# Three of the seven block products of q and k split a second time, in a two-layer graph network on one core

## The chip, the core and the metric

The kernel runs on one core of a Trainium2 chip. The metric is device time in microseconds (us). The kernel before takes 2371.41 us, the median of three runs (2370.97 to 2373.28). TensorE (PE) does matrix products into PSUM, VectorE (DVE) and ScalarE (ACT) work on SBUF and PSUM, GpSimd (POOL) on SBUF, and SyncE (SP) issues nearly all DMAs. Each engine works through its own queue in order.

## What is computed

128 graphs of 128 nodes with 512 features, in float32. Cut to what matters:

```python
# layer 0: attention over 8 heads of 64 features, masked by adj
q, k, v = x @ Wq + bq, x @ Wk + bk, x @ Wv + bv
scores = einsum('bqhd,bkhd->bhqk', q, k) / sqrt(64) + (1 - adj) * -1e9
out = einsum('bhqk,bkhd->bqhd', softmax(scores), v)
x = layernorm(x + out @ Wo + bo)
# layer 1: additive attention
h = x @ W;  s1, s2 = h @ a[:512], h @ a[512:]
e = leaky_relu(s1[:, :, None] + s2[:, None, :]) * adj
x = layernorm(x + elu(softmax(e) @ h + beta * h))
```

## The kernel before

**Tiling.** A batch is one graph; two batches are a group g (64 groups, b0 and b1), two groups a step of four batches. The five products with a 512x512 weight are done by groups in halves: weight and x are cut into 2x2 blocks, and seven block products with sums of blocks on both sides take the place of eight (Strassen's scheme in Winograd's form). The weights' sums are made once (`weight_sum`, L220), those of x, of the attention's output and of layer 1's aggregate by GpSimd (`block_sum`, L260; tiles tx, tw, th). `product` (L300) does one of the seven. For q and k it covers two groups at once: four matmuls of 256 columns (L325). For v, w (the output product with Wo) and h (with W) it is two matmuls for one group (L318).

**Adding up.** Products 1, 6, 5, 3 accumulate in one PSUM tile (`main`), 7 and 4 in another (`side`), and 2 stands alone for q and k. Between them the running sum is read out: `take_part` (L364) copies it to SBUF on ScalarE (on VectorE for w, with the residual added), `add_block` (L380) adds a later part on VectorE. A product that accumulates further waits until the running sum has been read out.

**Attention.** `scores` (L388) makes q k^T, `mask` (L402) scales and masks it on VectorE into tile s, `row_max` (L411), `exps` (L415) and `row_inv` (L424) prepare the softmax, `normalise` (L428) writes it on ScalarE into a second tile sb, laid out in 32-column pieces. It is transposed by a write to DRAM (`attn_write`), a read back in blocks (`attn_read`, tile ab) and a 32x32 block transpose on VectorE (`turn_attn`, L458). `attend` (L467) multiplies by v (PSUM tile po), `attend_evict` (L479) brings it to SBUF (oT).

**Layer 1.** Statistics of the first norm (`bn_stats`, `bn_aggr`, `inv_std` with a power on GpSimd), `row_product` (L518, two per batch, for s1 and s2), `norm_c` (L536, VectorE, into tile x1), the edge weights (`edge`, `leaky`, `edge_exp`, `weights`), `aggregate` (L655, PSUM tile pz, four matmuls of 128 columns), the h products, and ELU: `elu_exp` (ScalarE), `elu_max` and `elu_sum` (VectorE, into tile u), the last norm `norm_f` and `store`.

**x and the weights.** `load_blocks` (L78) fetches x in 32-row pieces, `turn_x` (L246) transposes it by 32x32 blocks on VectorE. It reads every fourth feature (a stride of four elements), so that wq, wk and wv can be loaded with four whole rows per partition (`load_turned`, L103, one DMA each).

**What sets the order.** No scheduler: `rows` (L765), `last_rows` (L908) and the lists in `other` (L1043) give every piece of every group a place, `lay` (L1235) shifts it by STEP for each pair of groups, and the pieces are issued sorted by place (L1284). The order on each engine is thus written out by hand; waits come from the tiles' uses.

Of the kernel before, what the change touches and what calls it, by code (L numbers as in the profile page):

```python
# [13 lines left out]
P = 128  # L14
Q = 32
# [3 lines left out]
STEP = 72.624  # L19
# [3 lines left out]
def gnn_two_layers(  # L23
# [70 lines left out]
    def load_x(b):  # L94
        t = wk2.tile([P, D], F32, tag="x", name=f"x_{b}", bufs=4)
        nc.sync.dma_start(out=t, in_=x[b])
        return t
# [5 lines left out]
    def load_turned(t, src):  # L103
        nc.sync.dma_start(out=t, in_=src.rearrange("(p m) f -> p m f", m=NC))
# [15 lines left out]
    load_turned(wq_sb, wq)  # L120
# [28 lines left out]
    nc.gpsimd.memset(mhalf, -0.5)  # L149
    bq_c, bk_c, bv_c = (bias_c[:, i * NC : (i + 1) * NC] for i in range(3))  # L150
# [7 lines left out]
    def load_later():  # L158
        nc.gpsimd.dma_start(out=adj_sb, in_=adj)
        later["beta"] = broadcast(cpool, beta, 1, "beta_b")  # L160
        later["bo"] = broadcast(cpool, bo, D, "bo_b")
        for j in range(2):
            a_j = a1[j * D : (j + 1) * D].rearrange("f o -> (f o)")
            later["a", j] = broadcast(wk2, a_j, D, "uf")
# [18 lines left out]
    def wa_column(j, c):  # L183
        t = wk2.tile([P, D], F32, tag="u", name=f"wa_t_{j}_{c}", bufs=1)
# [35 lines left out]
    def weight_sum(name, n, eng):  # L220
# [5 lines left out]
        s2, s3, s4 = (sums[name][:, i] for i in range(3))  # L226
        if n == 3:
# [7 lines left out]
        left[name] = {1: a11, 2: a12, 3: s4, 4: a22, 5: a21, 6: s2, 7: s3}  # L235


    right, tx, qT, kT, vb, y, hp, main, side, oT, zT, xr = ({} for _ in range(12))
# [7 lines left out]

    def turn_x(g, t):
        nc.vector.transpose(  # L248
            xT_all[:, :, t, g % 2, :].rearrange("p m (b r) -> p b m r", r=Q),
            xblk[g][:, t].rearrange("p b (c m) -> p b m c", c=Q),  # L250
        )
# [7 lines left out]

    def block_sum(name, g, n):  # L260

        if name == "x":
            b11, b12, b21, b22, (t1, t2, t3, t4) = x_blocks(g % 2)
        else:
            src = oT if name == "w" else zT
            b11, b12 = src[g * G][:, :2], src[g * G + 1][:, :2]
            b21, b22 = src[g * G][:, 2:], src[g * G + 1][:, 2:]
            if (name, g) not in tx:
                tx[name, g] = grp.tile(
                    [P, 4, 2, N], F32, tag=f"t{name}", name=f"t{name}_{g}", bufs=1  # L270
                )
            t1, t2, t3, t4 = (tx[name, g][:, i] for i in range(4))
        to, a, b = {1: (t1, b12, b11), 2: (t2, b22, t1), 3: (t3, b22, b12), 4: (t4, b21, t2)}[n]
        nc.gpsimd.tensor_tensor(to, a, b, ALU.subtract)  # L274
        if name != "x":
            right[name, g] = {1: b11, 2: b21, 3: b22, 4: t4, 5: t1, 6: t2, 7: t3}

    def factor(name, g, n):

        if name in "qkv":  # L280
            b11, b12, b21, b22, (t1, t2, t3, t4) = x_blocks(g % 2 if name == "v" else None)
            return {1: b11, 2: b21, 3: b22, 4: t4, 5: t1, 6: t2, 7: t3}[n]
        if (name, g) in right:
            return right[name, g][n]

        src = oT if name == "w" else zT
        return {1: src[g * G][:, :2], 2: src[g * G][:, 2:]}[n]
# [52 lines left out]
    def whole(name, b):  # L340
        out = OUT[name]
        if b not in out:
# [18 lines left out]
    def plain_take(b):  # L361
        nc.vector.tensor_tensor(whole("w", b), pl["w", b], xr[b], ALU.add)

    def take_part(name, g, n, i, j):  # L364
# [5 lines left out]
        elif name == "w":  # L370
            res = xr[g * G + j][:, i * HF : (i + 1) * HF]
            nc.vector.tensor_tensor(dst, src, res, ALU.add)  # L372
        else:
            for m in range(2):
                nc.scalar.activation(  # L375
                    dst[:, m, :], src[:, m, :], AF.Identity,
                    bias=BIAS[name][:, 2 * i + m : 2 * i + m + 1],
                )

    def add_block(name, g, n, i, j):  # L380

        src, dst = region(name, g, n), block(name, g, i, j)
        nc.vector.tensor_tensor(dst, src, dst, ALU.add)


    psc, s_t, nmax, rsum, rinv, sb, scr_t, ab = ({} for _ in range(8))
# [15 lines left out]
    def mask(b, j):  # L402
        if j == 0:
            s_t[b] = wk2.tile([P, H, N], F32, tag="s", name=f"s_{b}")
        nc.vector.scalar_tensor_tensor(  # L405
            s_t[b][:, j * HP : (j + 1) * HP, :], psc[b][j], SCALE,
            amask.rearrange("p (o n) -> p o n", o=1).broadcast_to([P, HP, N]),
            ALU.mult, ALU.add,
        )

    def row_max(b):  # L411
        nmax[b] = st.tile([P, H], F32, tag="nmax", name=f"nmax_{b}")
        nc.vector.tensor_reduce(nmax[b], s_t[b], AX.X, ALU.max, negate=True)  # L413

    def exps(b, k):  # L415
        if k == 0:
            rsum[b] = st.tile([P, H], F32, tag="rsum", name=f"rsum_{b}")
        for h in range(2 * k, 2 * k + 2):
            nc.scalar.activation(  # L419
                s_t[b][:, h, :], s_t[b][:, h, :], AF.Exp, bias=nmax[b][:, h : h + 1],  # L420
# [7 lines left out]
    def normalise(b, k):  # L428

        if k == 0:  # L430
            sb[b] = wk2.tile([P, 4, H, Q], F32, tag="sb", name=f"sb_{b}", bufs=1)
        for h in range(2 * k, 2 * k + 2):
            nc.scalar.mul(  # L433
                sb[b][:, :, h, :], s_t[b][:, h, :].rearrange("p (b c) -> p b c", c=Q),
                rinv[b][:, h : h + 1],
            )

    def attn_write(b):
        scr_t[b] = scr.tile([P, 4, H * Q], F32, tag="scr", name=f"scr_{b}")
        nc.sync.dma_start(out=scr_t[b], in_=sb.pop(b).rearrange("p b h c -> p b (h c)"))  # L440
# [15 lines left out]
    attnT, po, x1, stats, mv, ve, rstd, s12, s12n = ({} for _ in range(9))  # L456

    def turn_attn(b, half):  # L458
        if half == 0:
# [54 lines left out]
    def inv_std(g, name, i=None):  # L514
        t, r = pair(rstd, (name, g), f"rstd{name}"), part_of(i)
        nc.gpsimd.tensor_tensor(t[:, r], ve[name, g][:, r], mhalf[:, r], ALU.pow)

    def row_product(b, j):  # L518
# [3 lines left out]
        z = wk2.tile([P, D], F32, tag="u", name=f"ya_{b}_{j}", bufs=1)  # L522
# [794 lines left out]
```

## Time and profile before

One execution was profiled. Its span from the first to the last instruction is 2365.3 us; the time of that execution from outside is not listed, and the median of the runs, 2371.41 us, lies 6.1 us above the span.

| | us | share of the span | instructions |
|---|---|---|---|
| span of the profiled execution | 2365.3 | | 42947 |
| TensorE matmul busy | 2332.2 | 99% | 14129 |
| VectorE busy | 1923.8 | 81% | 4198 |
| ScalarE busy | 1494.1 | 63% | 5251 |
| GpSimd busy | 874.8 | 37% | 1044 |
| granted TensorE clock | 0.998 of full | | |

How to read the profile: a row of a group gives line, engine, operation, written and read tiles, shape and count; then busy time in all, mean ns of one, and the idle time just before them with what ended it. A float32 matmul stands in the trace as two records, each with its own weight load. Records of TensorE overlap: what a matmul costs is the distance from its start to the next one's start. Busy time of an engine that doesn't bound the end costs nothing.

### The profile page before, as it was taken

How to read it: one execution, taken by the hardware profiler on the slowest of the kernel's cores; microseconds unless marked ns; L12 is line 12 of the kernel's file. 1: busy time of each engine (PE TensorE's matmuls, PEld its weight loads, DVE VectorE, ACT ScalarE, POOL GpSimd, SP SyncE). 2: the span in 40 equal slices, each digit the busy share in tenths (PEclk: the TensorE clock that was granted, in tenths of full speed). 3: DMA queues.
4: the chain of work that ended last, by engine and by line, in shares of the span. 5: the costliest groups of instructions: out<-in, count | busy, mean ns of one | idle time of the engine just before them, and what ended most of it. 6: DMA issues, size and time to landing. Idle time of an engine off the chain costs nothing.

```text
span 2365.3 us, 42947 instructions
## 1 busy us (share of the span) xinstructions
PE 2332.2 (99%) x14129; PEld 2045.5 (86%) x14129; DVE 1923.8 (81%) x4198; ACT 1494.1 (63%) x5251; POOL 874.8 (37%) x1044
## 2 busy tenths in 40 slices
PE   9999999999999999999999999999999999999997
PEld 8888888888888888888888888888888888888885
DVE  7778887888887888878888887888788887888887
ACT  4565665766756666667566576665666666756665
POOL 6333333343333343433333333333334343333331
PEclk9999999999999999999999999999999999999999
DMA  5433434334334343343343443433434434344332
GB/s 184 123 94 110 128 91 127 109 103 134 97 112 131 99 117 119 97 132 101 111 133 91 120 124 94 130 114 94 136 97 114 124 96 128 101 112 135 92 125 76
DMA packets 255942, 269.31 MB, mean 114 GB/s; under 512 B 57356, under 2 KB 204568, under 8 KB 255336
## 3 DMA queue, kind: packets, MB, share of 16 engines
q1 hardware_dynamic: 254160, 265.06, 38.3%
q8 instruction: 112, 1.84, 0.3%
q14 instruction: 110, 0.90, 0.1%
q10 hardware_dynamic: 1256, 0.66, 0.1%
q0 software_dynamic: 304, 0.85, 0.1%
HBM read 157.62 MB, written 108.85 MB: 113 GB/s over the span
## 4 chain that ended last, share of the span: by engine, by line
PE 86%; DMA 6%; DVE 3%; SPq 3%; issue 1%; ACT 1%; DVEq 0%; ACTq 0%; POOLq 0%; POOL 0%
PE p1w L318 12%; PE p1q L325 9%; PE p1k L325 9%; PE p1v L318 9%; PE p1h L318 8%; PE psc L397 5%; PE pz L660 5%; PE p7q L325 5%; PE p7k L325 5%; DMA ab<-scr 5%; PE p7w L318 4%; PE po L472 4%; PE p7v L318 4%; PE p7h L318 3%; PE p2q L325 2%; PE p2k L325 2%
## 5 line engine op out<-in xcount | busy, mean ns | idle before, releaser
L419 ACT ACTIVATE s<-s,nmax 128x128 f32<-128x128 f32 x1024 | 397.1, 392 | 109.0 <-DVE nmax L413 109.0
L433 ACT ACTIVATE sb<-s,rinv 128x128 f32<-128x128 f32 x1024 | 323.0, 394 | 1.4 <-DMA scr<-sb 1.3
L484 ACT ACTIVATE oT<-po,bias_c 128x128 f32<-128x128 f32 x512 | 145.9, 380 | 222.6 <-PE po L472 222.1
L375 ACT ACTIVATE kT<-p1k,bias_c 128x256 f32<-128x256 f32 x256 | 106.2, 466 | 182.9 <-PE p1k L325 182.9
L372 DVE TENSOR_TENSOR w<-p1w,x 128x256 f32<-128x256 f32 x252 | 105.9, 420 | 140.9 <-PE p1w L318 140.6
L453 POOL TENSOR_TENSOR x<-x,bo_b_in 128x512 f32<-128x512 f32 x128 | 175.6, 1373 | 71.5 <-DMA x<-in_x_dram 71.1
L405 DVE SCALAR_TENSOR_TENSOR s<-psc,amask 128x512 f32<-128x512 f32 x256 | 165.7, 670 | 41.8 <-PE psc L397 40.1
L462 DVE STREAM_TRANSPOSE attnT<-ab 128x512 f32<-128x512 f32 x256 | 169.7, 691 | 34.2 <-DMA ab<-scr 34.2
L419 ACT ACTIVATION_READ_ACCUMULATOR s<-s,nmax 128x1 f32 x1024 | 195.3, 191 | 0.0
L369 ACT COPY h<-p1h 128x256 f32<-128x256 f32 x252 | 94.5, 375 | 157.8 <-PE p1h L318 151.8
L523 DVE SCALAR_TENSOR_TENSOR ya<-w,wa_row 128x512 f32<-128x512 f32 x256 | 191.8, 749 | 2.3
L274 POOL TENSOR_TENSOR tx<-xT 128x256 f32<-128x256 f32 x128 | 92.4, 734 | 188.4 <-DVE xT L248 164.0
L413 DVE TENSOR_REDUCE nmax<-s 128x8 f32<-128x1024 f32 x128 | 155.6, 1216 | 2.3
L274 POOL TENSOR_TENSOR th<-zT 128x256 f32<-128x256 f32 x63 | 46.1, 731 | 273.3 <-ACT zT L667 273.3
L248 DVE STREAM_TRANSPOSE xT<-xblk 128x512 f32<-128x512 f32 x128 | 141.9, 1110 | 5.4 <-DMA xblk<-in_x_dram 5.3
L472 PEld LDWEIGHTS po<-attnT,v 128*64 128x64 f32 x2048 | 109.8, 137 | 38.2 <-DVE attnT L462 15.9
L472 PE MATMUL po<-attnT,v 128*64 128x128 f32 x2048 | 132.3, 277 | 10.1 <-DVE attnT L462 9.9
L660 PEld LDWEIGHTS pz<-attT,x 128*128 128x128 f32 x1024 | 130.5, 193 | 9.8 <-issue 4.9
L369 ACT COPY v<-p1v 128x256 f32<-128x256 f32 x256 | 91.7, 371 | 70.2 <-PE p1v L318 66.1
L660 PE MATMUL pz<-attT,x 128*128 128x128 f32 x1024 | 131.5, 277 | 4.1 <-DVE attT L600 2.7
L318 PE MATMUL p1v<-wv_sb,xT 128*128 128x256 f32 x512 | 133.9, 385 | 0.0
L318 PE MATMUL p1w<-wo_sb,oT 128*128 128x256 f32 x504 | 132.5, 385 | 0.0
(681 smaller groups left out, 6153.3 us busy)
## 6 DMA issues: line engine op xcount, KB each, us to landing
scr<-sb SPq DMA_DIRECT2D x128, 512.0 KB
ab<-scr SPq DMA_DIRECT2D x512, 128.0 KB
x<-in_x_dram SPq DMA_DIRECT2D x128, 256.0 KB
out_dram<-u SPq DMA_DIRECT2D x127, 256.0 KB
xblk<-in_x_dram SPq DMA_DIRECT2D x252, 128.0 KB
pb<-s2d SPq DMA_DIRECT2D x62, 128.0 KB
attd<-att SPq DMA_DIRECT2D x62, 128.0 KB
ab<-attd SPq DMA_DIRECT2D x248, 32.0 KB
```

The lines of the kernel that those rows point to most:

```text
L318: nc.tensor.matmul(out, b[:, c, :], a[:, c, :], start=first and c == 0, stop=(c == 1), skip_group_check=True,)
L325: nc.tensor.matmul(out[:, m, :], a[:, c, m * P : (m + 1) * P], b[:, c, :], start=first and m == 0 and c == 0, stop=(c == 1), skip_group_ch ...
L369: nc.scalar.copy(dst, src)
L405: nc.vector.scalar_tensor_tensor(s_t[b][:, j * HP : (j + 1) * HP, :], psc[b][j], SCALE, amask.rearrange("p (o n) -> p o n", o=1).broadcast ...
L413: nc.vector.tensor_reduce(nmax[b], s_t[b], AX.X, ALU.max, negate=True)
L419: nc.scalar.activation(s_t[b][:, h, :], s_t[b][:, h, :], AF.Exp, bias=nmax[b][:, h : h + 1], accum_out=rsum[b][:, h : h + 1],)
L433: nc.scalar.mul(sb[b][:, :, h, :], s_t[b][:, h, :].rearrange("p (b c) -> p b c", c=Q), rinv[b][:, h : h + 1],)
L453: nc.gpsimd.tensor_tensor(xr[b], xr[b], later["bo"], ALU.add)
L462: nc.vector.transpose(attnT[b].rearrange("p h (a r) -> p a h r", r=Q)[:, rows], ab[b].rearrange("p a (h c) -> p a h c", c=Q)[:, rows],)
L472: nc.tensor.matmul(po[b][j * HD : (j + 1) * HD, m, :], vb[b][:, h * HD : (h + 1) * HD], attnT[b][:, j * HP + m, :], start=True, stop=True,)
L523: nc.vector.scalar_tensor_tensor(z, y[b], 1.0, wa_row[j], ALU.mult, ALU.mult, accum_out=s12[g][:, i, j : j + 1])
L660: nc.tensor.matmul(pz[b][:, c, :], x1[b][:, c * P : (c + 1) * P], attT[g][:, i, :], start=True, stop=True,)
```

## The change

- **Second level.** From group 2 on, products 2, 3 and 4 of q and k are each computed by seven products of half-size blocks: 128x128 weights (`weight_inner`, made once) and 128 columns of x (`inner_sums`, three GpSimd instructions per product and step, in tile xi with two buffers). They go into a PSUM tile pi of their own, in four chunks, and after each chunk `inner_add` adds two of its four parts (one after the third) to q or k in SBUF. Because product 3 no longer ends the running sum and 4 no longer ends the side sum, `take_more` copies the sum after 5 to the place of 3, and `add_more` adds 7 to the place of 4.
- **One tile per batch from x to output.** The tile that `fetch_x` fills holds the residual, then y (`take_part` for w adds in place), then the normalised x1, then u, and is stored. Tag "x" has ten buffers, shared with the scratch of `row_product` and `wa_column`; tags u, uf and x1 are gone. sb is gone too: the mask writes s in 32-column pieces and `normalise` works in place. Some small tiles share buffers (ea, et, pa).
- **Moved work.** `norm_c` goes from VectorE to ScalarE, with its bias (minus mean times rstd) from two more GpSimd instructions in `inv_std`. ELU becomes max(h,0) + exp(-relu(-h)): a Relu is added on ScalarE, and `elu_sum` goes from VectorE to GpSimd. The scale 1/8 goes from the mask to q's evictions and additions.
- **Weights by feature rows.** `load_turned` loads rows in the order of features, in 8 DMAs for wq and 4 each for wk and wv, and `turn_x` reads contiguous features.
- **Replanned.** Every list of places is replaced; STEP is 71.1556 instead of 72.624.

```diff
-STEP = 72.624
+STEP = 71.1556
+S_BUFS = 2
+XI_BUFS = 2
...
-        t = wk2.tile([P, D], F32, tag="x", name=f"x_{b}", bufs=4)
+        t = wk2.tile([P, D], F32, tag="x", name=f"x_{b}", bufs=10)
...
-    def load_turned(t, src):
-        nc.sync.dma_start(out=t, in_=src.rearrange("(p m) f -> p m f", m=NC))
+    def load_turned(t, src, step=NC):
+        for m in range(0, NC, step):
+            for a in range(4):
+                nc.sync.dma_start(
+                    out=t[a * Q : (a + 1) * Q, m : m + step, :],
+                    in_=src.rearrange("(a m c) f -> a c m f", a=4, c=Q)[a][:, m : m + step],
+                )
...
-            xblk[g][:, t].rearrange("p b (c m) -> p b m c", c=Q),
+            xblk[g][:, t].rearrange("p b (m c) -> p b m c", c=Q),
...
+    INNER = {'q': (2, 3, 4), 'k': (2, 3, 4)}
+    TO = {2: (0, 0), 3: (0, 1), 4: (1, 0)}
...
+    def weight_inner(name, n, eng):
+        a = left[name][n]
+        a11, a21, a12, a22 = a[:, 0, :N], a[:, 0, N:], a[:, 1, :N], a[:, 1, N:]
+        t = cpool.tile([P, 3, N], F32, tag=f"wi_{name}{n}", name=f"wi_{name}{n}")
+        eng.tensor_tensor(t[:, 1], a11, a21, ALU.subtract)
+        eng.tensor_tensor(a21, a21, a22, ALU.add)
+        eng.tensor_tensor(t[:, 0], a21, a11, ALU.subtract)
+        eng.tensor_tensor(t[:, 2], a12, t[:, 0], ALU.subtract)
+        wi[name, n] = (a11, a12, t[:, 2], a22, a21, t[:, 0], t[:, 1])
+
+    def inner_sums(g, n):
...
+        b = factor("q", g, n)
+        t = wk2.tile([P, 4, N], F32, tag="xi", name=f"xi{n}_{g}", bufs=XI_BUFS)
+        nc.gpsimd.tensor_tensor(
+            t[:, :2], b[:, :, N:], b[:, 0, :].rearrange("p (s n) -> p s n", s=2), ALU.subtract
+        )
+        nc.gpsimd.tensor_tensor(t[:, 2], b[:, 1, N:], t[:, 0], ALU.subtract)
+        nc.gpsimd.tensor_tensor(t[:, 3], b[:, 1, :N], t[:, 2], ALU.subtract)
...
+    def deep(name, g, n):
+        return g > 1 and n in INNER.get(name, ())
+
+    def inner_product(name, g, n, k):
...
+        if k == 0:
+            pi[name, g, n] = ps_mm.tile([P, 4, N], F32, tag="mm", name=f"pi{n}{name}_{g}")
+        for i, r in (((1, 1), (7, 2), (2, 0)), ((6, 1), (4, 2)), ((5, 1),), ((3, 1),))[k]:
+            pair_of = wi[name, n][i - 1], xi[g, n][i - 1]
+            nc.tensor.matmul(
+                pi[name, g, n][:, r, :], *(pair_of[::-1] if name == "v" else pair_of),
+                start=(i == 1), stop=True, skip_group_check=True,
+            )
+
+    def inner_add(name, g, n, k):
...
+        dst = dst[:, first : first + 1 if k == 2 else first + step + 1 : step, :]
+        if name == "q":
+            nc.vector.scalar_tensor_tensor(dst, src, SCALE, dst, ALU.mult, ALU.add)
+        else:
+            nc.vector.tensor_tensor(dst, src, dst, ALU.add)
...
+        if name == "c":
+            m = pair(nmc, g, "nmc")[:, r]
+            nc.gpsimd.tensor_tensor(m, mv["c", g][:, r, 0], t[:, r], ALU.mult)
+            nc.gpsimd.tensor_tensor(m, zero[:, r], m, ALU.subtract)
...
-        z = wk2.tile([P, D], F32, tag="u", name=f"ya_{b}_{j}", bufs=1)
+        z = wk2.tile([P, D], F32, tag="x", name=f"ya_{b}_{j}", bufs=10)
...
-        x1[b] = wk2.tile([P, D], F32, tag="x1", name=f"x1_{b}", bufs=4)
-        nc.vector.tensor_scalar(
-            x1[b], y[b], mv["c", g][:, i, 0:1], rstd["c", g][:, i : i + 1],
-            ALU.subtract, ALU.mult,
+        x1[b] = y.pop(b)
+        nc.scalar.activation(
+            x1[b], x1[b], AF.Identity, bias=nmc[g][:, i : i + 1], scale=rstd["c", g][:, i : i + 1]
         )
...
+    def elu_max(b):
+        u[b] = x1.pop(b)
+        nc.vector.scalar_tensor_tensor(u[b], hp[b], 0.0, u[b], ALU.max, ALU.add)
+
     def elu_exp(b):
...
+        eh[b] = hp.pop(b)
+        nc.scalar.activation(eh[b], eh[b], AF.Relu, scale=-1.0)
+        nc.scalar.activation(eh[b], eh[b], AF.Exp, scale=-1.0)
...
-        nc.vector.scalar_tensor_tensor(u[b], hp.pop(b), 1.0, u[b], ALU.min, ALU.add)
+        nc.gpsimd.tensor_tensor(u[b], u[b], eh.pop(b), ALU.add)
```

The second level takes its inputs so that VectorE and TensorE alternate on a tile pi: chunk k+1 accumulates into a part that `inner_add` k has just read.

## The prediction

> **What bounds the kernel now.** I read the profiled execution from the whole to the part: the busy shares, the chain that ended last, the stretches, the waits of TensorE, then single groups. First the page's shares and chain:
>
> ```profile
> PE 2332.2 (99%) x14129; PEld 2045.5 (86%) x14129; DVE 1923.8 (81%) x4198; ACT 1494.1 (63%) x5251; POOL 874.8 (37%) x1044
> ...
> PE 86%; DMA 6%; DVE 3%; SPq 3%; issue 1%; ACT 1%; DVEq 0%; ACTq 0%; POOLq 0%; POOL 0%
> ```
>
> TensorE is busy for 99% and is 86% of the chain; no other engine is above 81%. But busy spans overlap, so the next two views ask whether it really has no holes. The stretches (columns: us, PE busy, PEld, DVE, ACT, POOL, clock, DMA share, GB/s), and the longest waits of PE:
>
> ```profile
> 1139.40:1212.00 72.60, 72.42 (x442) 63.73 (x441) 59.21 (x131) 46.62 (x164) 26.99 (x33) 1.00 0.38 113
> 2237.00:2365.30 128.30, 110.29 (x626) 90.65 (x624) 103.29 (x255) 77.43 (x250) 32.75 (x41) 0.96 0.31 103
> ...
> PE po L472 <- DVE attnT L462: 9.9, 18, 1.2
> PE pz L660 <- DVE attT L600: 2.7, 1, 2.7
> ```
>
> A step of four batches takes 72.6 us and TensorE is idle for 0.2 of it. Idle time sits in the last 128 us (18.0) and in waits of attention for its transposed weights (9.9 in all). So time is the sum of TensorE's slots, and an edit counts by what it does to that sum, as long as the others keep up. Slots are read from starts in PE's timeline, not from durations:
>
> ```profile
> 1158.27 1.89 PE L325 MATMUL p7k<-tx,s_k 128*128 128x256 f32 x8
> 1160.00 1.89 PE L325 MATMUL p1k<-tx,wk_sb 128*128 128x256 f32 x8
> 1161.72 1.05 PE L660 MATMUL pz<-attT,x 128*128 128x128 f32 x8
> 1162.62 1.89 PE L325 MATMUL p1q<-xT,s_q 128*128 128x256 f32 x8
> ```
>
> A matmul is two records. A q or k product (four matmuls of 256 columns) starts 1.73 us after the one before it; the four 128-column matmuls of pz, each with new 128x128 weights, take 0.89: 0.432 and 0.222 each.
>
> **TensorE, the part that pays.** Products 2, 3 and 4 of q and k, four matmuls of 256 columns, become seven of 128 from the second pair of groups on: 7 x 0.222 = 1.554 instead of 1.727, 0.173 less. There are 6 of them in each of 31 steps: 186 x 0.173 = 32.2 us. Every other matmul stays, in number and shape.
> The Trainium skill (TensorE: Matmul & The Clock Gate, Back-to-back issue gap) speaks against this: weight loads set the spacing too, 81 ns at 128 columns and 131 at 512. An estimate from it, linear between the two: 98 at 256, so half the columns save only 17%, a deep product costs 7 x 0.83 / 4 = 1.45 of a plain one, and the sum is 186 x 0.78 = 144 us worse. The pz row has exactly the new shape and fresh weights each time, and shows 0.51 of the 256-column slot. I take the row.
>
> **The round trips that come with it, on the path.** A deep product is issued in four chunks of 3, 2, 1 and 1 matmuls into one PSUM tile. After each, VectorE adds two (once one) of its 128-column parts to q or k, and the next chunk writes into a part just read. So PE's chunk k+1 waits for VectorE's addition k; behind it, in order, is everything of PE. The new order puts other matmuls between. Priced by the slots above, the shortest covers are: 2.19 us (q, 3, first to second), 2.20 (k, 4, third to fourth), 2.39 (k, 2), 2.42 (q, 4); after the last chunk, two attends of 0.95 precede the scores (1.90). An addition is about 0.41 (row below), so some 1.5 us remain for VectorE's queue: one long instruction (row_max 1.22) fits, two don't. Best case 0; worst about 1 us a step, 31. I take 3: VectorE runs ahead of TensorE here as before.
>
> **VectorE's sum.** Rows for the additions, for x's transpose, and for a transpose with contiguous reads:
>
> ```profile
> L383 DVE TENSOR_TENSOR w<-p7w,w 128x256 f32<-128x256 f32 x126 | 52.5, 417 | 3.3 <-PE p7w L318 2.2
> L383 DVE TENSOR_TENSOR qT<-p7q,qT 128x512 f32<-128x512 f32 x64 | 44.0, 687 | 39.0 <-PE p7q L325 33.6 <-ACT qT L375 5.3
> L248 DVE STREAM_TRANSPOSE xT<-xblk 128x512 f32<-128x512 f32 x128 | 141.9, 1110 | 5.4 <-DMA xblk<-in_x_dram 5.3
> L462 DVE STREAM_TRANSPOSE attnT<-ab 128x512 f32<-128x512 f32 x256 | 169.7, 691 | 34.2 <-DMA ab<-scr 34.2
> ```
>
> Added: 186 deep products x (3 x 0.415 + 0.30) = 287 (0.30 for 128 columns, between 0.27 on the line through 417 and 687, and L641's 0.346); inner weight sums, 24 x 0.3 = 7. Product 4's addition becomes the second one of product 7, so only product 2's goes: 62 x 0.69 = -43. The ELU sum (L680, 126 x 0.677) goes to POOL: -85. The normalisation (L540, 128 x 0.536 to 0.737) goes to ACT: -81. x's transpose reads contiguously, because the weights now carry the feature order: 0.69, like L462, 128 x 0.42 = -54 (0 if the stride isn't the cause: then it costs no path, only cover). The mask writes in 32-column pieces and the row maximum reads them; the shapes aren't in the trace: between 0 and +0.1 each, 0 to 38, I take 0. Sum +31: 1955.
>
> **POOL, ACT and the shared port.** POOL gains the ELU sum (126 x 1.28, L453's median: 161), 93 inner sums of a 256- and two 128-column instructions (0.73 + 2 x 0.46: 153) and 130 tiny ones for -mean x rstd (0.2 to 0.9, I take 0.5: 65): 1254, 54%. ACT gains the normalisation (128 x 0.806, as L744) and a Relu ahead of each Exp (126 x 0.626): 1676, 72%. Both stay beside TensorE. The normalisation now waits on ACT for POOL's power (L516, up to 1.12) and two of the tiny ones; behind it stand evictions that free PSUM, and the order puts at least one group of evictions between. But the Trainium skill (SBUF — State Buffer, Who interferes with whom) says that a VectorE instruction with two SBUF inputs and a POOL instruction block each other whole. The trace agrees: sorted by whether a POOL instruction lay beside it, L612 takes 337 or 815 ns, L618 421 or 814, L523 668 or 805, while additions from PSUM take 409 or 411. The new additions read PSUM, so they are free of it. By the rule at its worst, the 704 two-input instructions left x 54% x 0.73 give 277; less the waits already in the rows (61, next sentence) VectorE is at 2171, 93% of the new span: nearly the bound. By the rows the excess was 21 + 28 + 12 = 61 us at 37% POOL, so +28 at 54%: 1983, 85%. I take the rows; what POOL delays first is the batch statistics that wait for its ELU sum, with w's additions queued behind on VectorE, covered by 2.1 us of matmuls and more.
>
> **Buffers and queues.** One tile per batch lives from x's load to the store, ten buffers, which the row products' scratch shares: a fetch now waits on SP for a scratch product or a store to end, with attention's writes queued behind. Attention's own tile is normalised in place (two buffers, until its write has landed). The number of DMAs a step on SP is unchanged. In the order, the VectorE work between a batch's reciprocal and its turned weights goes from 10–17 to 8–22 us: the odd groups gain 2 to 7, the even ones lose up to 8. So of the 9.9 us of waits I take 4 away (0 to 8). Head: the three turned weights are 16 SP issues instead of 3, at 0.46 each (four x blocks: 1.86), so wq's last issue moves from 3.4 to about 6.3 us; it had landed at 10.0, beside the first product at 10.3, which waits for the bias rows. And six row products of the attention vector (0.69 to 1.8 each) stand ahead of k's weight sums. 0 to 7, I take 2. Tail: reordered, 18 us idle to win from and the same chain of small steps: -8 to +5, I take -3.
>
> **Sum.** -32.2 + 3 - 4 + 2 - 3 = -34.2. The profiled span of 2365.3 becomes 2331; the median shown, 2371.4, lies 6.1 above that span, which no part of the change touches: 2337.
>
> **Rivals.** (a) *The round trips stall.* Near the scores VectorE serves additions of six deep products, statistics and row products, and POOL is active beside. If two long instructions or a locked pair stand ahead of each second addition, PE loses 0.4 to 0.5 us at some six of the 18 covers: 2.7 us a step, 31 x 2.7 = 84, less 34: 2420, slower. It decides at 34 / 31 = 1.1 us a step. For it: the 1.5 us margins, and nothing on PE can overtake. Against: VectorE is idle for 13 us of each step now. (b) *Half of that:* 0.7 us a step, +22: 2359, still faster; above 0.95 it is within 0.2%, which is about what a measurement of this kernel can tell from no change. (c) *The new order also closes the old holes:* all attention waits and 10 us of the tail go: 2322. (d) *The change doesn't reach TensorE's sum*, if 128-column slots in short chunks take more than pz's: at 0.247 nothing is saved, 2369; nothing in the row suggests it, and it is counted in (b) and "same".
>
> **Chances.** Forecast (2326 to 2350) 0.60; (c) 0.12; (b) 0.14, 0.04 of it within 0.2%; (a) 0.14. Faster 0.82, same 0.04, slower 0.14. Range 2316 to 2368: it takes in most of (c) and (b).
>
> **What would show it.** Right: a step of about 71.5 us between the same scores, pi rows at 111 ns a record, no wait of PE on q's or k's additions above a few us in all, x's transpose at 0.69. Wrong: waits "pi <- DVE qT or kT" or "psc <- DVE" of tens of us (a); pi rows well above 111 (d); PE idle in the first 60 us above 10 (head).

## The result and the profile after

The changed kernel takes 2342.4 us, the median of four runs (2342.09 to 2343.9); the kernel before took 2371.62 beside it. The ratio is 0.9875, interval 0.9861 to 0.9889: 1.25% faster. The forecast was 2337, in a range of 2316 to 2368. The direction and the main term hold. The start costs far more than forecast and the steady state gains more, so the total is nearer to the forecast than its terms are.

First the page of the kernel after, its busy shares and its chain:

```profile
PE 2305.1 (98%) x15245; PEld 2059.6 (88%) x15245; DVE 1910.0 (82%) x4651; ACT 1643.8 (70%) x5505; POOL 1208.3 (52%) x1580
...
PE 90%; DVE 5%; ACT 2%; DMA 1%; issue 1%; POOL 1%; SPq 0%; POOLq 0%; DVEq 0%; ACTq 0%
```

TensorE is busy for 27 us less, in 1116 more instructions, and still sets the time. The stretches of the kernel after (us, then PE, PEld, DVE, ACT, POOL busy, clock, DMA share, GB/s) are the first 60 us, a step of four batches, and the end:

```profile
0.00:60.00 60.00, 44.97 (x234) 38.47 (x235) 34.44 (x63) 15.06 (x47) 23.02 (x32) 0.94 0.56 146
1139.00:1210.18 71.18, 71.18 (x478) 64.20 (x477) 58.19 (x145) 51.30 (x172) 37.00 (x49) 1.00 0.38 116
2209.00:2340.30 131.30, 117.78 (x712) 97.20 (x710) 106.98 (x276) 96.25 (x302) 65.60 (x80) 0.99 0.33 108
```

A step takes 71.18 us, and TensorE has no hole in it at all; between 350 and 2033 us the trace lists no wait of PE. But the first 60 us hold 15.0 us of idle PE, where the kernel before has 5.0. The slots, from PE's timeline of the kernel after:

```profile
1160.65 1.89 PE L335 MATMUL p1q<-tx,wq_sb 128*128 128x256 f32 x8
1162.38 0.38 PE L440 MATMUL pi3k<-xT,s_k 128*128 128x128 f32 x2
1162.60 0.39 PE L440 MATMUL pi3k<-xi,wi_k 128*128 128x128 f32 x2
...
1163.05 0.39 PE L440 MATMUL pi2k<-xT,wi_k 128*128 128x128 f32 x2
1163.27 1.89 PE L335 MATMUL p7q<-tx,s_q 128*128 128x256 f32 x8
```

A 128-column matmul of the second level starts every 0.22 us (112 ns a record, the median of 2199), as pz's did; the whole products keep 1.73.

To say where time went I cut each execution at the start of the scores of batches 0, 20 and 112. By batch 0 TensorE has done the same work in both kernels. By batches 20 and 112 the new order has done 28 more records of v's products and 4 fewer of h's, 24 x 0.216 = 5.2 us more work; so 5.2 us of the second stretch belong to the last one.

| us | to scores 0 | to 20 | to 112 (one step of four) | to the end | span |
|---|---|---|---|---|---|
| before | 36.3 | 337.7 | 1672.4 (72.71) | 318.8 | 2365.3 |
| after | 49.9 | 346.0 | 1637.2 (71.18) | 307.2 | 2340.3 |
| difference | +13.6 | +8.3 | -35.2 (-1.53) | -11.6 | -25.0 |

With these 5.2 us in their place, the change wins 41.6 us in the steady state and at the end (35.2 + 6.4), and gives back 16.7 up to batch 20 (13.6 + 3.1). The time from outside is 1.8 us above the span here.

The head's lines: first GpSimd's loads in the kernel before (its first, and the two broadcasts of the attention vector), then the same three in the kernel after.

```profile
12.62 0.71 POOL L159 DMA_DIRECT2D adj_sb<-in_adj_dram  x1
...
14.38 1.06 POOL L109 DMA_DIRECT2D uf_in<-in_L_gnn_a_dram  x2
```

```profile
1.40 0.73 POOL L169 DMA_DIRECT2D adj_sb<-in_adj_dram  x1 [0.26 <-issue]
...
3.57 1.08 POOL L116 DMA_DIRECT2D oT_in<-in_L_gnn_a_dram  x2
```

VectorE's first sum of wq in the kernel before, then VectorE in the kernel after (its first work):

```profile
10.01 0.95 DVE L228 TENSOR_TENSOR s_q<-wq_sb 128x512 f32<-128x512 f32 x1 [0.43 <-DMA wq_sb<-in_L_gnn_Wq_dram]
```

```profile
9.76 1.30 DVE L261 STREAM_TRANSPOSE xT<-xblk 128x512 f32<-128x512 f32 x2 [9.76 <-DMA xblk<-in_x_dram]
14.93 0.69 DVE L239 TENSOR_TENSOR s_q<-wq_sb 128x512 f32<-128x512 f32 x1 [3.87 <-DMA wq_sb<-in_L_gnn_Wq_dram]
15.54 0.70 DVE L261 STREAM_TRANSPOSE xT<-xblk 128x512 f32<-128x512 f32 x1
...
20.23 0.70 DVE L261 STREAM_TRANSPOSE xT<-xblk 128x512 f32<-128x512 f32 x1
```

And TensorE's waits in the kernel after, the four longest (in total, times, longest):

```profile
PE p2q L335 <- DVE bias_c L159: 4.4, 1, 4.4
PE early L152 <- DMA bias_rows<-in_L_gnn_bv_dram: 3.0, 1, 3.0
PE early L148 <- POOL ident masks.py:199: 2.6, 1, 2.6
PE p7q L335 <- POOL tx L293: 2.5, 1, 2.5
```

The reader is to see three things: 0.85 MB of loads, nearly all broadcasts, now goes out at the very start beside x and wq; even the first half of wq is there only at 14.93 (all of it at 10.01 before); and the turns of x for group 0 stand behind the sum that waits for it, so GpSimd's block sums and the products on them come later still. The wait put down to bias_c ends at 16.43 with VectorE's work behind that sum, the turn at 15.54 and the bias at 16.17; wq's second half is there by 16.41 too, and this trace doesn't say which of them came last.

### The profile page after: what moved, and what is told of

Its sections match the earlier page's. It is cut to its first block, busy times and chain, and to the rows that moved or that the text cites. A ratio compares the mean times of both kernels' runs of the same rounds, so it can differ in the third digit from the quotient of the medians.

```text
span 2340.3 us, 46764 instructions
## 1 busy us (share of the span) xinstructions
PE 2305.1 (98%) x15245; PEld 2059.6 (88%) x15245; DVE 1910.0 (82%) x4651; ACT 1643.8 (70%) x5505; POOL 1208.3 (52%) x1580
## 4 chain that ended last, share of the span: by engine, by line
PE 90%; DVE 5%; ACT 2%; DMA 1%; issue 1%; POOL 1%; SPq 0%; POOLq 0%; DVEq 0%; ACTq 0%
PE p1v L328 11%; PE p1h L328 11%; PE p1w L328 11%; PE p1k L335 7%; PE p1q L335 7%; PE po L572 5%; PE psc L499 5%; PE pz L764 5%; PE p7w L328 4%; PE p7h L328 4%; PE p7v L328 4%; PE p7k L335 2%; PE p7q L335 2%; PE pi4q L440 2%; PE pi4k L440 2%; PE pi3k L440 2%
## 5 line engine op out<-in xcount | busy, mean ns | idle before, releaser
L536 ACT ACTIVATE s<-s,rinv 128x128 f32<-128x128 f32 x1024 | 330.3, 395 | 16.9 <-DVE rinv L531 16.4
L293 POOL TENSOR_TENSOR tw<-oT,oT 128x256 f32<-128x256 f32 x63 | 45.9, 728 | 401.0 <-ACT oT L584 399.5
L784 POOL TENSOR_TENSOR x<-x,h 128x512 f32<-128x512 f32 x126 | 162.9, 1293 | 107.7 <-ACT h L781 86.5
L627 DVE SCALAR_TENSOR_TENSOR ya<-x,wa_row 128x512 f32<-128x512 f32 x256 | 204.3, 798 | 2.1
L507 DVE TENSOR_TENSOR s<-psc,amask 128x512 f32<-128x512 f32 x256 | 169.4, 675 | 18.1 <-PE psc L499 14.9
L771 ACT COPY zT<-pz 128x512 f32<-128x512 f32 x128 | 74.5, 585 | 126.0 <-PE pz L764 125.9
L384 DVE TENSOR_TENSOR x<-p1w,x 128x256 f32<-128x256 f32 x252 | 103.1, 409 | 61.6 <-PE p1w L328 56.4
L499 PE MATMUL psc<-kT,qT 64*128 64x128 f32 x2048 | 133.0, 279 | 0.4 <-DVE s L507 0.4
L499 PEld LDWEIGHTS psc<-kT,qT 64*128 64x128 f32 x2048 | 120.2, 188 | 12.7 <-issue 11.2
```

Of the source, the lines that this page charges most:

```text
L499: nc.tensor.matmul(psc[b][j][:, m, :], qs[feats, m, :], ks[feats, m, :], start=True, stop=True,)
L507: nc.vector.tensor_tensor(s_t[b][:, :, j * HP : (j + 1) * HP, :].rearrange("p b h c -> p h b c"), psc[b][j].rearrange("p h (b c) -> p h b ...
L536: nc.scalar.mul(s_t[b][:, :, h, :], s_t[b][:, :, h, :], rinv[b][:, h : h + 1])
L627: nc.vector.scalar_tensor_tensor(z, y[b], 1.0, wa_row[j], ALU.mult, ALU.mult, accum_out=s12[g][:, i, j : j + 1])
```

## The experiments

My theory was: the time is TensorE's slots plus holes; the second level gives the slots, and the head's holes come from wq's late arrival and VectorE's order there. The rivals: the gain is the new order's, not the second level's; and the round trips are near their limit. Each run is the changed kernel with the edit shown. Results by stage are in one table behind the last run; small differences are read from it, since the runs of the kernel before spread by 4 to 9 us within one set. The table has one execution of each run. Runs 1, 7, 8, 9 and 11 leave the order of the head's loads and turns alone, and start wq's first sum at 14.5 to 16.1 and the first scores at 49.9 to 52.1: a step of 2 us at the head is not clear of that spread by itself.

**1. The second level alone taken out.**

```diff
-        if k == 0:
-            pi[name, g, n] = ps_mm.tile([P, 4, N], F32, tag="mm", name=f"pi{n}{name}_{g}")
+        if k:
+            return
+        out = pi[name, g, n] = ps_mm.tile([P, 2, HF], F32, tag="mm", name=f"pi{n}{name}_{g}")
+        a, b = left[name][n], factor(name, g, n)
+        for m in range(2):
+            for c in range(2):
+                nc.tensor.matmul(
+                    out[:, m, :], a[:, c, m * P : (m + 1) * P], b[:, c, :],
...
```

`inner_add` then adds the whole 512 columns at k = 0; `inner_sums` and `weight_inner` do nothing.

> Products 2, 3 and 4 of q and k are done whole (8 records, 1.73 us) into the same tile, in the same place of the order, and added in one instruction; the sums of the second level are left out, everything else is as in the changed kernel. Theory (the time is TensorE's slots plus its holes, and the steady state has no hole): 186 x 0.173 = +32 us of slots, holes as they were: 2374 us (2371 to 2378), TensorE busy 2337. Rival 1 (the gain is due to the rest of the change, the new order and the lighter VectorE): 2342 to 2352. Rival 2 (the second level brought hidden waits of its own, in the head too): 2355 to 2365.

Measured: 2372.2 us, ratio to the kernel before 1.0018 (1.0008 to 1.0027), span 2370.4, and the page of this run:

```profile
PE 2336.5 (99%) x14129; PEld 2046.9 (86%) x14129; DVE 1771.0 (75%) x4069; ACT 1643.7 (69%) x5505; POOL 1032.7 (44%) x1301
```

The theory's number. Spans differ by 30.1 us; 186 x (1.727 - 14 x 0.112) is 29.6. The second level is worth more than the whole net gain. But the step, 72.17, is still 0.54 below the kernel before, without any second level: something else in the change closes holes.

**2 to 4. The head by parts: turns first, wq in four DMAs, weights strided.**

The first edit is in group 0's list of places.

```diff
-            -30.8778, -82.6249, -45.3036, -0.6412, -25.3126, -41.9185, 0.362, -66.7049, -26.6618,
+            -30.8778, -84.6, -84.55, -0.6412, -25.3126, -41.9185, 0.362, -66.7049, -26.6618,
```
```diff
-    load_turned(wq_sb, wq, 2)
+    load_turned(wq_sb, wq)
```
```diff
-        for m in range(0, NC, step):
-            for a in range(4):
-                nc.sync.dma_start(
...
+        nc.sync.dma_start(out=t, in_=src.rearrange("(p m) f -> p m f", m=NC))
...
-            xblk[g][:, t].rearrange("p b (m c) -> p b m c", c=Q),
+            xblk[g][:, t].rearrange("p b (c m) -> p b m c", c=Q),
```

> The two turns of x for group 0 stand ahead of q's first weight sum on VectorE, not one behind it and one behind four sums and four inner sums. Theory (the order makes the head's waits): the block sums of x on GpSimd begin about 4 us earlier (16.8 instead of 20.9), the holes before p1q and p7q (1.63 and 2.53) close: 2338 us (2335 to 2340). Rival (wq's landing at 14.9 and k's weights behind the six column products set the head): 2341 to 2343.

> wq is loaded by 4 DMAs of 256 KB in place of 8 of 128 KB, order and bytes as they were. Rival A (SyncE's number of issues makes wq late): four issues fewer, wq and all that is behind it on the queue 3 to 4 us earlier, 2338 us (2336 to 2340). Rival B (the pieces of 2 KB and the bytes set the rate): landing within 1 us of before, 2341 to 2344, since now q's first half no longer comes ahead of the second.

> Weights strided over the features again, one DMA each of wq, wk and wv, and the turn of x reads with stride as in the kernel before; all else as in the changed kernel. Theory (steady state full, head slow by its loads): the turns take 1.07 us instead of 0.70, some 47 us more of VectorE, all hidden: steady state unchanged within 1 us; wq lands at about 10 instead of 14.9: 2336 us (2333 to 2340). Rival (the lighter turn is what closed the steady holes): 8 to 11 us of holes come back between batches 20 and 112, 2343 to 2350.

Measured: 2339.5, 2347.1 and 2345.8 us. Turns first gains 2.8 in the span, in the theory's range; the block sums are done at 15.1 us and no longer waited for, but p2q now waits for wq until 17.99. Four DMAs cost 5.2 us: both my rivals missed it. The number of issues isn't the price: with four, wq's last issue goes out at 8.1 instead of 12.6, and yet the first sum waits to 18.88. With eight, q's first half lands ahead of its second. Strided weights come in one DMA, and yet wq is there only at 14.0, and the first scores at 49.7: going back to one DMA does not mend the head. I had expected 2336 and was wrong. The turns of group 0 stand behind wq's sum in this run too, which can hide a part of what the earlier landing is worth. The turn does take 1.10 us instead of 0.70, and these 51 us of VectorE are hidden in the steady state (71.18 in both), so the lighter turn didn't close the holes.

**5 and 6. The head's order, then the broadcasts.** Both have the turns first. Seven more `wa_column` follow the one shown, and the columns' tiles are taken where they were. The second edit is in run 6 only.

```diff
-    at(-62.7872, load_k_and_v)
+    at(-84.53, load_k_and_v)
...
-    at(-80.746, load_weight, w1_sb, w1)
+    at(-62.7, load_weight, w1_sb, w1)
...
-    at(-61.8116, make_mask)
+    at(7.9, make_mask)
...
-    at(-33.2916, wa_column, 0, 2)
+    at(7.640, wa_column, 0, 2)
```
```diff
-    at(-103.9883, load_later)
+    at(-0.1, load_later)
```

> Order at the head alone: the turns of group 0 first, the instruction that holds k's and v's loads ahead of q's first sum on VectorE (it stood behind it), w's load behind k's and v's, the mask and the eight products for w's attention columns behind k's sums. The broadcasts stay where they are. In the run with the turns alone TensorE starts at 17.99 and has then 1.7 us of half clock and holes of 0.97 and 0.93 before the first scores. Theory (by now: what is left at the head is wq's late landing, not VectorE's order): only those two holes can go, 2338 us (2336 to 2340). Rival (VectorE's order and k's load held back): 2332 to 2335.

> As the run before it, and the five loads that GpSimd issues (0.85 MB, nearly all of it broadcasts to 128 partitions) stand behind the block sums of x, as in the kernel of the start, where they went out at 12.6 to 15.4; in the changed kernel they go out at 1.4 to 4.6, beside x and wq. Theory (they share the DMA engines with wq and x and make these late): wq lands at 10 to 12 instead of 16 to 18, and the first products follow: 5 to 7 us less than the run before it, 2332 us (2329 to 2334). Rival (the 2 KB pieces of wq make it late, whatever else runs): within 2 us of the run before it.

Measured: 2338.9 (span 2335.7) and 2334.3 us (span 2332.7; ratio 0.9865, 0.985 to 0.988). VectorE in the first and in the second of them, q's first two sums:

```profile
12.77 1.20 DVE L244 TENSOR_TENSOR s_q<-wq_sb 128x512 f32<-128x512 f32 x1 [1.92 <-DMA wq_sb<-in_L_gnn_Wq_dram]
...
15.06 0.71 DVE L246 TENSOR_TENSOR wq_sb<-wq_sb 128x512 f32<-128x512 f32 x1 [0.49 <-DMA wq_sb<-in_L_gnn_Wq_dram]
```

```profile
10.22 0.78 DVE L244 TENSOR_TENSOR s_q<-wq_sb 128x512 f32<-128x512 f32 x1 [0.18 <-DMA wq_sb<-in_L_gnn_Wq_dram]
...
12.85 0.76 DVE L246 TENSOR_TENSOR wq_sb<-wq_sb 128x512 f32<-128x512 f32 x1 [1.24 <-DMA wq_sb<-in_L_gnn_Wq_dram]
```

With nothing but the broadcasts moved, both halves of wq land 2.2 to 2.5 us earlier and the first scores 3.0: less than the 5 to 7 I expected. The direction is settled: on the same chip, every execution of the second (2334.0 to 2335.0) is faster than every one of the first (2337.4 to 2340.1). For the first of the two the time lies in the theory's range: the order on VectorE, with k's and w's loads, gave 1.8, which is within the head's spread.

**7 and 9. The two moved instructions back on VectorE, with and without the second level.**

```diff
-        nc.scalar.activation(
-            x1[b], x1[b], AF.Identity, bias=nmc[g][:, i : i + 1], scale=rstd["c", g][:, i : i + 1]
-        )
+        nc.vector.tensor_scalar(
+            x1[b], x1[b], rstd["c", g][:, i : i + 1], nmc[g][:, i : i + 1], ALU.mult, ALU.add
+        )
...
-        nc.gpsimd.tensor_tensor(u[b], u[b], eh.pop(b), ALU.add)
+        nc.vector.tensor_tensor(u[b], u[b], eh.pop(b), ALU.add)
```

> The first layer's normalisation and the sum behind the ELU go back to VectorE (the changed kernel has them on ScalarE and GpSimd); all else as in the changed kernel. VectorE +128 x (0.35 to 0.5) + 128 x (0.65 to 0.8) = some 130 to 165 us, to 87 to 89% of the span. Theory (steady state has slack and its holes were closed by the order): steady step 71.2 us as before, 2342 to 2345. Rival (it was these moves that closed the holes of the attention waits): 8 to 12 us come back, 2350 to 2355.

> The second level left out of q and k (the three products whole, one addition each), and the first layer's normalisation and the ELU's sum on VectorE: VectorE 1771 + 150 = 1920 us, near the kernel of the start. The run with the second level and these two on VectorE took 2378.5, the run without the level and with the two moved away 2372.2. Theory A (the moved instructions closed the holes of the steady state, whatever the products are): step of four batches 72.17 + 0.44 = 72.6 us, 2382 to 2390. Theory B (the moves only pay for the second level's additions, 155 us of VectorE; without these nothing waits): step 72.17, 2372 to 2376.

Measured: 2378.5 us (1.0055, 1.004 to 1.007) and 2398.3 us (1.013, 1.0115 to 1.0145). My theory of the first fell: slower than the kernel before, with VectorE at 87%. Its waits in the steady state:

```profile
PE p1w L328 <- DVE x L384: 4.1, 21, 0.3
PE p1h L328 <- ACT h L382: 1.4, 1, 1.4
```

And in the second run, the longest of the steady state:

```profile
PE p1w L328 <- DVE x L384: 3.7, 19, 0.2
```

w's additions on VectorE now come too late for the next product. The step rises by 0.44 with the second level and by 0.43 without it, the step that theory A of the second run gave. But its mechanism, and that of the first run's rival, is not shown: what comes back are not the old holes. Before the change TensorE waited ahead of attend for the turned weights (9.9 us, in the prediction's lines); here, by the distances from start to start, all of the steady loss (9.9 and 10.0 us) stands ahead of w's product 1, and attend waits for nothing. So in this order the two instructions have no room on VectorE, with or without the second level's additions; that their move closed the old holes doesn't follow (the second run's total was beyond what I gave for it, too). Half of the first run's loss, and over a third of the second's, lies in the stretch up to batch 20: 20.7 and 10.2 us. Both have one wait of 5.4 us for h's evictions there, and 13.7 and 6.8 us at half clock behind their waits (last section).

**8 and 11. The same 558 idle VectorE instructions, in the round trips and elsewhere.** The edit of the first run; in the second the same instruction stands behind the statistics, the row products and every second edge sum.

```diff
+        if k < 3:
+            nc.vector.scalar_tensor_tensor(idle, ident, 1.0, ident, ALU.mult, ALU.mult)
```

> An idle VectorE instruction (128x128, two inputs, 0.28 us alone, up to 0.56 beside GpSimd) ahead of the first three additions of each product of the second level, 558 in all, 160 to 250 us more of VectorE (89 to 92%), all of it inside the round trips from TensorE to VectorE and back. Theory (the covers of 1.9 us and more hold with some to spare): 2342 to 2347. Rival (the round trips are near their limit, each delay shows): from 558 x 0.3 x 0.15 = 25 us up, 2367 and more.

> The same 558 idle instructions on VectorE (0.276 us each, 154 us) as in the run that had them in the round trips (2374.0), but spread behind the row products, the statistics and every second edge sum, 4.5 for each batch from batch 4 on. Theory (it is the delay in the round trip that hurts, queue time elsewhere is absorbed): 2342 to 2350. Rival (VectorE's load as such: at 86% each burst puts some addition behind its due time, wherever the time is spent): 2362 to 2376.

Measured: 2374.0 us (span +28.7) and 2451.0 us (span +113.9; 1.0347, 1.0329 to 1.0364). Both times the rival won, and the second ran past it. Waits of PE in the steady state, of the first run and of the second:

```profile
PE pi3q L441 <- DVE qT L471: 2.9, 19, 0.2
```

```profile
PE pi2k L441 <- DVE kT L471: 46.8, 22, 2.3
```

In the first, one idle instruction ahead of each addition is listed as 0.15 us at one round trip of a step, at the shortest cover of the prediction (q, 3: 2.19 us). The list is short of what a wait costs, as the record before it is drawn longer than its slot (1.89 us for 1.73 above). By the distances from start to start, TensorE loses 0.40 us a step there, 0.11 at q's product 4 and 0.07 at k's product 2: 0.58 of the 0.61 by which the step grows.

In the second, the same time behind the statistics and row products makes one wait of 2.1 to 2.3 us at a single place, k's product 2 (cover 2.39), and the step grows by 3.70. By the starts, 2.47 of it is this wait, and 0.81 stands in q's product 7 right behind, which often runs at half clock; 0.20 is at w's product 1 and 0.16 at k's product 4. Here it is followed by the next product at 1141.40, so product 7 takes 3.05 us instead of 1.73:

```profile
1137.76 0.80 PE L441 MATMUL pi2k<-xT,wi_k 128*128 128x128 f32 x2 [2.29 <-DVE kT L471]
1138.35 3.21 PE L335 MATMUL p7q<-tx,s_q 128*128 128x256 f32 x8
```

That is rival (a)'s mechanism, at covers that the prediction lists. No VectorE share tells it: both stand at 86%.

**10 and 12. A better head.** Both from run 6.

```diff
-    early = keep_busy(20, "early")
+    early = keep_busy(28, "early")
...
-            -30.8778, -84.6, -84.55, -0.6412, -25.3126, -41.9185, 0.362, -66.7049, -26.6618,
+            -30.8778, -84.6, -84.55, -0.6412, -25.3126, -41.9185, 0.362, -73.5, -26.6618,
```

Run 12 in addition moves the eight columns:

```diff
-    at(7.640, wa_column, 0, 2)
+    at(11.970, wa_column, 0, 2)
```

> As the run with the late broadcasts (2334.3), with q's product 1, which needs only the first half of wq, ahead of product 2, and 28 early products in place of 20, so that TensorE does not stand for 4.1 us and fall to half clock. Theory (2.5 us of waiting and 2 us of half clock at the start go straight to the end): 2330 us (2328 to 2332). Rival (the block sums of x or k's weights are late next): 2333 to 2335.

> As the run with q's product 1 first and the longer warm-up (2334.1, span 2330.5), with the eight products for w's attention columns behind k's addition of product 7 on VectorE, which they held up (TensorE waited 1.50 us for it ahead of k's product 4). Theory (each us of hole before the first scores is a us at the end): span 2329, 2332 us (2330 to 2334). Rival (the columns are then late for their turn on TensorE behind the first scores, and what is won is waited for there): no change.

Measured: 2334.1 us (2332.1 to 2336.9, span 2330.5; ratio 0.9859, 0.9845 to 0.9874) and 2337.3 us (span 2335.4). In the first, PE starts at 10.49 and never cools:

```profile
10.49 1.99 PE L340 MATMUL p1q<-xT,wq_sb 128*128 128x256 f32 x8
12.64 1.97 PE L340 MATMUL p2q<-xT,wq_sb 128*128 128x256 f32 x8 [0.16 <-issue]
15.10 1.97 PE L340 MATMUL p1q<-tx,s_q 128*128 128x256 f32 x8 [0.49 <-DVE s_q L248]
```

Its span is 2.2 us below run 6's, but its median is the same, in the rival's range. So both are some 8 us below the changed kernel by their medians, and the best of the runs made; they ran on other chips than it, and the intervals of their ratios overlap with its own. In the second neither held: the span is 4.9 us longer. The first scores start 0.7 earlier, but the eight columns now hold up additions of q and k that the rest of the scores of batches 0 and 1 need, and behind that wait TensorE runs at half clock from 42.2 to 49.0; the stretch up to batch 20 is 5.7 us longer.

```profile
PE psc L504 <- DVE qT L402: 3.0, 1, 3.0
```

| us | to scores 0 | to 20 | to 112 (one step) | to the end | span |
|---|---|---|---|---|---|
| after | 49.9 | 346.0 | 1637.2 (71.18) | 307.2 | 2340.3 |
| 1 one level | 49.9 | 347.9 | 1659.8 (72.17) | 312.8 | 2370.4 |
| 2 turns first | 47.9 | 345.5 | 1637.2 (71.18) | 306.8 | 2337.5 |
| 3 wq in four | 55.4 | 345.5 | 1637.2 (71.18) | 307.2 | 2345.5 |
| 4 strided | 49.7 | 347.7 | 1637.2 (71.18) | 308.5 | 2343.1 |
| 5 head's order | 46.0 | 345.6 | 1637.2 (71.18) | 306.9 | 2335.7 |
| 6 late broadcasts | 43.0 | 345.6 | 1637.2 (71.18) | 306.9 | 2332.7 |
| 10 product 1 first | 40.7 | 345.6 | 1637.2 (71.18) | 306.9 | 2330.5 |
| 12 columns later | 40.0 | 351.3 | 1637.2 (71.18) | 306.9 | 2335.4 |
| 7 back on VectorE | 51.1 | 366.7 | 1647.3 (71.62) | 315.4 | 2380.5 |
| 9 both | 50.7 | 358.1 | 1669.8 (72.60) | 318.7 | 2397.2 |
| 8 idle in trips | 50.3 | 351.5 | 1651.3 (71.79) | 315.9 | 2369.0 |
| 11 idle elsewhere | 52.1 | 356.6 | 1722.2 (74.88) | 323.3 | 2454.2 |

## Why the prediction was right, and where not

| term | forecast | measured | from |
|---|---|---|---|
| slots of the second level | -32.2 | -30.1 | run 1 against after |
| round trips | +3 | 0 | no PE wait from 350 to 2033 us |
| old holes of the steady state | -4 | -12.6 | -35.2 less run 1's share of it, -22.6 |
| head, to the first scores | +2 | +13.6 | table |
| from there to batch 20 | 0 | +5.0 | +8.3 less run 1's -1.9, less 5.2 of work done earlier |
| end | -3 | -0.8 | -11.6 less run 1's -5.6, plus these 5.2 |
| sum (spans) | -34.2 | -24.9 | |

That the total came so near is in part luck: up to batch 20 the change cost 16.6 us more than forecast, the old holes and the round trips came out 11.6 better, and 4.3 came back between span and time.

- **Slots.** Right. The row of pz held: 112 ns a record where the sum took 111. The estimate from the page's gap figures, 144 us worse, is refuted here for this shape and type.
- **Round trips.** The value was right, the reason half. "VectorE runs ahead of TensorE here" holds only for the load and order as planned: 154 us of idle instructions cost 28.7 or 113.9 us by where they stand. The chance of 0.14 for (a) was not too large; the decision lies in which long instructions stand ahead of which addition, and no average over a step shows that.
- **Old holes.** The right holes, and too little of them. Run 1 has the products of the kernel before, and its steady state is 12.6 us shorter; by the distances from start to start all of this stood ahead of attend, in the waits for turned weights that the list puts at 9.9 for the whole execution. The prediction took 4 of it away; all of it went. This part of rival (c) came true. It is not the lighter turn, the second level or the two instructions that left VectorE: runs 4, 1, and 7 and 9 undo them, and no wait of attend comes back in the steady state. Whether it is the new order or another part of the change, such as the softmax written in place, no run separates.
- **VectorE's sum.** All its instructions add up to 2165.7 us before and 2198.4 after, +32.7; the forecast was +31 and +28 of blocking. Blocking was over-priced: the row products, edge weights and ELU maxima take 55 us more, but the edge sums, the leaky step, `shift` and `scale_s` take 38 less. The busy time fell by 14 instead, since spans that follow each other without a hole overlap (the sum at 14.93 lasts 0.69, the next instruction starts after 0.61) and busy time counts the overlap once. The additions take 0.38 on the mean of both shapes, the turn 0.70, the mask 0.675 and the maximum 1.20, as taken. The tiny GpSimd products were over-priced: 0.2 us, not 0.5. Two of the lines:

```profile
L470 DVE TENSOR_TENSOR kT<-pi4k,kT 128x256 f32<-128x256 f32 (+1 forms) x124 | 47.7, 385 | 61.1 <-PE pi4k L440 58.9
L261 DVE STREAM_TRANSPOSE xT<-xblk 128x512 f32<-128x512 f32 x128 | 89.3, 698 | 9.8 <-DMA xblk<-in_x_dram 9.8
```

- **Head.** This is the large miss, and the failed step is "the three turned weights are 16 SP issues instead of 3": it looked for the cost in the price of an issue, and had wq's last one at 6.3. It went out at 12.6, but run 3 shows that earlier issues alone do not bring wq earlier. Runs 2, 5, 6 and 10 together take back 9.2 of the 13.6 us: 2.0 by the turns, 1.9 by the order of k's loads and of the attention columns, 3.0 by the broadcasts, 2.3 by product 1 first and the longer warm-up. The sum is well clear of the head's spread of 2.2, the single steps of about 2 us are not. No run accounts for the other 4.4 us. GpSimd's loads had been moved by 11 us, from behind the block sums to the front, and the prediction didn't follow each DMA that the replanning moved, on every queue. Its own sign for "wrong", PE idle above 10 in the first 60 us, showed it (15.0).
- **Up to batch 20.** +5.0 us that the forecast had not. PE idles 6.1 us between 50 and 350 us, against 1.2 before, in some ten waits, the longest (1.2 each) those of attend for ScalarE's evictions:

```profile
PE po L572 <- ACT oT L584: 2.5, 2, 1.2
```

  More load on VectorE lengthens this stretch too (by 20.7, 5.5 and 10.6 us in runs 7, 8 and 11). Which part of the plan makes the 5.0 was not tried; it stays open.
- **From span to time.** "6.1, which no part of the change touches" was a figure of that one execution. In every later run the profiled execution's own time lies some 1.8 above its span; so the profiled one of the kernel before took about 2367.1 by this, 4.3 less than the median beside it. The forecast's 2331 for the span missed by 9.3, and 4.3 of that came back here. By the medians the gain is 29.2 us, by the spans 25.0; the later sets of the kernel before have medians of 2367.4 to 2369.2.

## What to carry to other kernels

When one engine is full, count its slots from starts of a row with the same shape and fresh operands: that number held to 7%. What is gained there is kept only if the other engines' order leaves covers, so follow the few long instructions ahead of each short answer, not the engine's share. And for a replanned order, list every DMA with its new place on its own queue: the head alone gave back 13.6 of 41.6 us here.

## What the runs showed of the hardware

- A TensorE that waits cools. In the kernel after it waits from 8.9 to 11.9 and from 12.0 to 16.4 us, and its granted clock is half from 12.70 to 19.53; the first row is the stretch of 16 to 20 us there, the second the same stretch of run 10, which has no such wait (us, PE busy, clock, DMA share, GB/s).

```profile
16.00:20.00 4.00, 3.56 (x10) 0.56 0.91 275
```

```profile
16.00:20.00 4.00, 4.00 (x20) 1.00 1.08 224
```

  Product 2 takes 3.33 us from its start to the next one's instead of 1.73: 1.6 us lost beside the wait itself. The Trainium skill (TensorE: Matmul & The Clock Gate, What's actually happening) gives half rate after one idle window of some 3.4 us; the 3.41 us up to 12.70 hold 0.20 us of work, so this case agrees. The later waits of 1.6 and 2.5 us left no mark (clock 1.00 from 20 us on).
- A stretch need not be idle for that. In every trace here the clock stays half for a multiple of 3.41 us, but for what the end of the execution cuts off. Cut into stretches of that length, on the raster of its own changes, run 11 has this one, with 1.27 us of work, and the next (columns as above):

```profile
1134.20:1137.61 3.41, 1.27 (x9) 1.00 0.37 154
1137.61:1141.02 3.41, 3.26 (x9) 0.50 0.36 105
```

  Of the stretches at full clock in the 14 traces, all with up to 1.43 us of work are followed by half clock, none with 1.95 and more; between 1.58 and 1.85 both occur. So 13 of the 20 waits of 2.1 to 2.3 us at k's product 2 in run 11's steady state cost half clock behind them, and 7 don't: it depends on how a wait lies on the raster (the one that ends at 1213.11 is split by it, and the stretch to 1212.70 still holds 1.71 us of work). The measurement is stricter here than the idle window of the page.
- The same load of wq, one DMA issued at about 3.4 us in both, was there at 10.01 in the kernel before and at 14.04 in run 4, with q's own bytes unchanged. Other loads beside it differ there in more than the broadcasts; the pair that differs in these alone is runs 5 and 6 (12.77 and 10.22).
